# A post-norm decoder of two layers on one core: values, expert steps and the start of the self-attention in another order

## The chip, the core and the metric

The kernel runs on one core of one Trainium2 chip. The metric is the device time of one launch in microseconds; for this kernel it is the median of three runs. The core's engines run beside each other and meet at semaphores: TensorE (matmuls, results into eight PSUM banks of 2 KB per partition), VectorE, ScalarE, POOL (GpSimd) and SP (SyncE), which here only issues DMAs. DMAs are issued from SP's, ScalarE's and POOL's queues, each in the order of the program.

## What is computed

Four sequences of 512 tokens, width 256, pass through two layers; each sublayer is added to its input and normalized. All arithmetic is in 32-bit floats. Cut to what matters here:

```
x = LN(x + ttt(x))                       # layer 0: one inner SGD step per token
x = LN(x + attention(x, ctx, ctx, mask)) # one head, 1601 context rows per batch
p = softmax(x @ Wr + br); top 2 of 8 experts, weights w normalized to 1
x = LN(x + sum_k w_k * expert_k(x))      # expert: gelu(x Wi + bi) * sigmoid(x Wg + bg), Wo, LN
x = LN(x + causal_attention(x))          # layer 1: 16 heads of 16
Q, K = rope(x Wq + bq), rope(ctx Wk + bk); V = ctx Wv + bv
x = LN(x + softmax(Q K^T / 4) V Wo + bo) # 16 heads against 1601 context rows
x = LN(x + 0.5 * mlp(LN(x)))             # weights dequantized from integers
```

## The kernel before

The stages follow one another: layer 0's recurrence (to about 230 us of the span), its cross-attention (to about 530), the experts (to about 1001), layer 1's self-attention (to about 1440), its cross-attention (to about 2275) and the last block. Within a stage the program is a list of small Python closures called in an order written out by hand (`manual_schedule`), so each engine's instructions stand in that order, and a tile's reuse becomes a wait.

**The end of the first cross-attention.** While it ends, `value(b, k)` (L782) makes the value rows of layer 1's cross-attention for batches 2 and 3: 26 groups of 128 context rows, each of four TensorE instructions and a copy by ScalarE (L791). Two values share one two-bank tile of `wide()`; three such tiles and two one-bank tiles of `bank()` exist. When a batch's values are done, SP writes them to DRAM (`vd`, L793 to L797). Behind these on SP stand the loads of twelve weights and rows of layer 1 (L79, L92, L85), which go where the values lay, and then the experts' first rows `xb` (L922). Batch 3's routing and its scatter of rows run meanwhile.

**The experts.** `run` (L1110) goes through 19 blocks: eight "first" blocks, 256 rows of one expert each (weights loaded by SP), and eleven "more" blocks of two halves of 128 rows, each half of an expert found at run time (weights gathered by POOL). After `first_half` of a block, the second half of the block before follows, and then one step of the generator `attention_first` (L1019), which prepares layer 1: constants, tables, context columns of batch 0, masks. Attention needs, per batch, DRAM buffers `qd`, `ksd`, `kcd` of 32 rows per head, of which 16 come from projections and 16 are constants (`behind`, L877); these are copied from DRAM to DRAM on ScalarE's queue for all four batches, and then the mask rows (L1077). What is left of the generator runs behind the last block; then all engines meet at a branch (L1160).

**Behind the experts.** Eight PSUM banks are split into three of `spare()`, four of `one()` and one for the sums of weighted values. In this order come: gathers of batch 0's expert rows by POOL (L1223); values of batch 0 from context columns that lie in the tiles of queries and keys (`here=qt + kself`); two keys; values of batch 1 with the sums and the normalization of batch 0 (`add`) between the eighth and the ninth; transposes; keys; projection of first queries and keys (`self_rows`), which go through DRAM (L1202, L1205), since a row per head is to lie on other partitions; the rest of the keys. A key is copied by ScalarE (L1330) into one of four `raw` tiles and rotated by `rotated` (a shuffle and three products or sums). Rotated keys wait in the list `going` until `flush` issues their write.

Then come 16 self-attention units (batch, group of four heads) and 16 of cross-attention. A unit first runs its row maxima (`slot1`, TensorE and VectorE; 12 slots before the first unit), then scores, exponents and weighted sums. `extras[i]`, `quiet[i]` and `starts[i]` are lists of other closures that unit i runs between its own. The order before the first unit is:

```
for f in keys0[0:2] + values1[:8] + add + values1[8:] + turn + keys0[4:6]:
    f()
for f in (k0_, q0_, rows0, *keys0[2:4], *keys0[6:8], *self_values(0)):
    f()
cosT = const(p4c, "c_cos", [P, S2], nc.sync)
sinT = const(p4c, "c_sin", [P, S2], nc.sync)
flush(0)
```

`k0_`, `q0_`, `rows0` are the first half of batch 0's keys and queries and the loads of their rows; `k1_`, `q1_`, `rows1` the second half, which runs in unit 0.

Of the kernel before, what the change touches and what calls it, by code (L numbers as in the profile page):

```python
# [9 lines left out]
F32 = mybir.dt.float32  # L10
# [7 lines left out]
P = 128  # L18
# [7 lines left out]
NH, HD = 16, 16  # L26
# [13 lines left out]
def decoder(ctx: ExitStack, tc: tile.TileContext, a: dict, out: bass.AP):  # L40
# [14 lines left out]
    def wide():  # L55
        return psum["A"].tile([P, 2, 512], F32, tag="wide", name="wide")
# [571 lines left out]
    with tc.tile_pool(name="p2", bufs=2) as p2, ExitStack() as ordered:  # L628
# [135 lines left out]


        xaV = weight(p2, "xaV")
        values, places, halves = [], {}, []

        def rows_of_values(first):

# [10 lines left out]

        def value(b, k):  # L782
            kn = kn_of(k)
            if not halves or len(halves) == 2:
                halves[:] = [wide()]
            else:
                halves.append(halves[0])
            ps = halves[0][:, len(halves) - 1, :D]
            mm(ps[:kn], [(ctxTs[b][:, c, k * P : k * P + kn], xaV[:, c, :]) for c in range(2)])
            dst = places[b, k][:kn, : NH * VW].rearrange("p (h r) -> p h r", r=VW)  # L790
            nc.scalar.copy(dst[:, :, :HD], ps[:kn].rearrange("p (h r) -> p h r", r=HD))  # L791
            if (b, k) == (2, 8):
                nc.sync.dma_start(vd[2][:, : 9 * VROW], big_of(2, 0, 9))  # L793
            if (b, k) == (3, NKT - 1):
                nc.sync.dma_start(vd[3], big_of(3, 0, NKT))
            if (b, k) == (2, NKT - 1):
                nc.sync.dma_start(vd[2][:, 9 * VROW :], big_of(2, 9, NKT))  # L797

        def big_of(b, k0, k1):
            first = places[b, k0]  # L800
            return bass.AP(first.tensor, first.offset, [first.ap[0], [1, (k1 - k0) * VROW]])
# [72 lines left out]
    def by_head(t):  # L874
        return t.rearrange("(h r) n -> h r n", r=32)

    def behind(t, rows):  # L877

        nc.scalar.dma_start(by_head(t)[:, HD:, :], a[rows].rearrange("(h r) n -> h r n", r=HD))

    def group_tiles(pool, name, n):
        return [
# [11 lines left out]
    with tc.tile_pool(name="p3", bufs=2) as p3, ExitStack() as ordered:  # L894
# [124 lines left out]
        def attention_first():  # L1019
# [24 lines left out]
                    nc.scalar.dma_start(t, a[name][:, k0 : k0 + kw])  # L1044
                ready["turn", i] = pair
            yield
            for b in range(B):
                behind(qd[b], "c_rowq")
                behind(ksd[b], "c_rowks")
                yield  # L1050
            for b in range(B):
                behind(kcd[b], "c_rowkc")
                yield
            ngs = ready["ngs"] = []
            for i in range(2 * NT):
                t = p4a.tile([P, 4, 32], F32, tag=f"ng{i}", name=f"ng{i}")
# [7 lines left out]
            for c, k0 in enumerate(range(0, S2, 401)):  # L1064
# [8 lines left out]
                nc.sync.dma_start(mrow[:, k0 : k0 + kw], mf)  # L1073
                nc.vector.tensor_reduce(any_[:, c : c + 1], mf, AX.X, ALU.max)
                yield
            for b in range(B):
                nc.scalar.dma_start(  # L1077
                    by_head(kcd[b])[:, HD + 4, :], mrow[4 * b].partition_broadcast(NH)
                )
            yield  # L1080
            left = p3.tile([4 * B, 1], F32, tag="left", name="left", bufs=1)
            nc.vector.tensor_reduce(left, any_, AX.X, ALU.max)
# [57 lines left out]
                next(work, None)  # L1140
            second_half(blocks[-1], None, outs)

        order = "ffmfmfmmfmfmmfmfmm" + "m" * 1
        counts = {"f": iter(range(E)), "m": iter(range(NDYN // 2))}
        blocks = [({"f": "first", "m": "more"}[k], next(counts[k])) for k in order]
        def beside():
# [25 lines left out]
    with ExitStack() as s4:  # L1172
# [14 lines left out]
        def spare():  # L1187
            return ps2.tile([P, 512], F32, tag="s2", name="s2")

        def one():  # L1190
            return spare() if alone else ps1.tile([P, 512], F32, tag="one", name="one")

        diagq, later_, qt, kself, ngs, vself = (
            ready[k] for k in ("diagq", "later", "qt", "ks", "ngs", "vself")
# [67 lines left out]
            fetch = [lambda h=h: fetched(h) for h in range(2)]  # L1262
            return fetch, [lambda t=t: (added(t), stats(t)) for t in range(NT)] + ends, turns

        def self_rows(b, c):


            def item(name, dram, scale):
                ps = one()
                mm(ps, [(W[name][:, i, c * P : (c + 1) * P], xT[b][:, i, :]) for i in range(2)])  # L1270
                t = raw_tile()
                nc.scalar.activation(t, ps, AF.Identity, scale=scale)
                to_rows(dram, c, 0, S, t)

            def rows():
                for g in (2 * c, 2 * c + 1):
                    from_rows(kself, ksd[b], g)
                    from_rows(qt, qd[b], g)

            return [lambda: item("qkvK", ksd[b], 1.0), lambda: item("qkvQ", qd[b], QS)], rows  # L1280
# [40 lines left out]
        def context(b, keys, values, here=None):  # L1321


            def key(src, i, c, eng):
                flush(1)
                k0, kw = chunks[i]
                ps = one()
                mm(ps[:, :kw], [(W["xaK"][:, h, c * P : (c + 1) * P], src()[h][:, :kw]) for h in range(2)])
                raw = raw_tile()
                nc.scalar.activation(raw[:, :kw], ps[:, :kw], AF.Identity, bias=bkc[:, c : c + 1])  # L1330
                rotated(raw, kw, slice(k0, k0 + kw), eng, ready["turn", i] if here else None)
                going.append(lambda: to_rows(kcd[b], c, k0, kw, raw[:, :kw]))

            def value(src, k):
                kn, c0 = kn_of(k), (k % 4) * P
                ps = one()[:, :D]
                mm(ps[:kn], [(src()[c][:, c0 : c0 + kn], W["xaV"][:, c, :]) for c in range(2)])
                dst = vals[b % 2][:kn, k, : NH * VW].rearrange("p (h r) -> p h r", r=VW)
                nc.scalar.copy(dst[:, :, :HD], ps[:kn].rearrange("p (h r) -> p h r", r=HD))

            items = []
            for i in sorted({*keys, *values}):
                if here is None:
                    src = lambda n=len(stream): chunk(n)
                    stream.append((b, i))
                else:
                    src = lambda i=i: here[2 * i : 2 * i + 2]
                eng = nc.gpsimd if here is None else nc.vector
                if i in keys:
                    items += [lambda s=src, i=i, c=c: key(s, i, c, eng) for c in range(2)]  # L1350
                if i in values:
                    items += [lambda s=src, k=k: value(s, k) for k in range(4 * i, min(4 * i + 4, NKT))]
            return items
# [379 lines left out]
                starts[i + 1 + g].append(lambda b=b, g=g: from_rows(kcross, kcd[b], g))  # L1733


        fetch, add, turn = combined(0)
        values1 = context(1, (), range(4))
        keys1 = context(1, range(4), ())
        chunk(0)
        vals.append(values_tile(p4c, "v1", NKT))  # L1740
        for f in fetch:
            f()
        for f in first_sums:
# [2 lines left out]
            f()  # L1746
        nc.scalar.preload_act_table_set(EXP_AND_LN)

        keys0 = context(0, range(4), (), here=qt + kself)
        (k0_, q0_), rows0 = self_rows(0, 0)  # L1750
        (k1_, q1_), rows1 = self_rows(0, 1)

        for f in keys0[0:2] + values1[:8] + add + values1[8:] + turn + keys0[4:6]:
            f()
        for f in (k0_, q0_, rows0, *keys0[2:4], *keys0[6:8], *self_values(0)):
            f()
        cosT = const(p4c, "c_cos", [P, S2], nc.sync)
        sinT = const(p4c, "c_sin", [P, S2], nc.sync)
        flush(0)
        for i, (n0, n1) in enumerate(((0, 4), (4, 6), (6, 7), (7, 8))):  # L1760
            extras[i] = ([k1_, q1_, rows1] if i == 0 else []) + keys1[n0:n1] + extras[i]
        later = [context(2, range(4), ()), context(3, range(4), ())]
        for b in (2, 3):
            starts[index[b - 1, 1, True]].append(
# [2 lines left out]
        for b, work in enumerate(later):  # L1767
            for g in range(NG):
                n = -(-len(work) // (NG - g))
                extras[index[b, g, True]] += work[:n]  # L1770
                work = work[n:]

        nothing = lambda: None
        quiet[index[1, 0, True]].append(bias_out)
# [228 lines left out]
```

## Time and profile before

| | us |
|---|---|
| median of three runs (2403.08 to 2413.41) | 2409.47 |
| profiled execution | 2402.61 |
| its span, first to last instruction | 2400.8 |
| TensorE busy | 2275.6 |
| TensorE busy of the 420 us from 590 to 1010 (experts) | 394.1 |
| TensorE busy of the 50 us from 1010 to 1060 | 38.6 |
| TensorE busy of the 60 us from 1060 to 1120 | 59.0 |
| TensorE busy of the 1060 us from 1240 to 2300 | 1053.4 |

The span is that of one execution taken by the hardware profiler. An entry of a timeline gives start and length in us, the engine, the line of the kernel, the operation with its output and inputs, how many instructions are merged in it, and in brackets how long the engine was idle before it and what ended that. A row of stretches gives, for each engine, its busy time and the number of instructions. The granted clock is the share of full speed at which TensorE was allowed to run; over the whole span it was 0.97.

### The profile page before, as it was taken

The page shows a single profiled execution, that of the slowest core. Times are in us where ns is not written, and L with a number is a line of the kernel's source. Part 1 is how long each engine was busy: PE and PEld are TensorE (multiplying, and loading weights), DVE is VectorE, ACT ScalarE, POOL GpSimd, SP SyncE. Part 2 cuts the span into 40 slices and gives each one's busy share as a digit, 9 for nine tenths or more (in the row PEclk, how much of TensorE's full clock was granted, in tenths as well). Part 3 has the DMA queues.
Part 4 walks back from the last instruction along what each step waited for, and adds up shares of the span by engine and source line. Part 5 has one row for each costly group of instructions (what it writes and reads, how often), then busy time and mean ns, then how long its engine had stood idle before and what let it go on. Part 6 is the DMA issues. An engine that isn't in the chain of part 4 may idle for free.

```text
span 2400.8 us, 36163 instructions
## 1 busy us (share of the span) xinstructions
PE 2275.6 (95%) x14448; PEld 1289.9 (54%) x14448; DVE 1239.0 (52%) x2928; ACT 1064.2 (44%) x2103; POOL 360.0 (15%) x373
## 2 busy tenths in 40 slices
PE   7899999968999999889999999999999999999998
PEld 4767577757898988643333334333333333333266
DVE  1433234431333334356666667666766776677234
ACT  1111122213554545324555553655656566566730
POOL 1010001130122223225230010120122010000000
PEclk9999999988999999989999998999999999999999
DMA  8400311135887867341210210111110010100000
GB/s 304 173 0 1 132 55 46 45 137 178 321 333 308 338 258 300 132 147 50 67 49 27 77 64 1 37 33 59 56 58 28 25 60 15 54 11 20 30 10 27
DMA packets 77100, 244.14 MB, mean 102 GB/s; under 512 B 11640, under 2 KB 34686, under 8 KB 64638
## 3 DMA queue, kind: packets, MB, share of 16 engines
q1 hardware_dynamic: 60126, 137.41, 16.7%
q0 software_dynamic: 13632, 89.32, 9.7%
q10 hardware_dynamic: 3168, 15.03, 1.8%
q8 instruction: 116, 1.90, 0.3%
q14 instruction: 58, 0.48, 0.1%
HBM read 196.12 MB, written 56.77 MB: 105 GB/s over the span
## 4 chain that ended last, share of the span: by engine, by line
PE 50%; DVE 1%; ACT 1%; issue 0%; DVEq 0%; ACTq 0%
PE s L1458 23%; PE po L1485 12%; PE one L202 11%; PE s L202 2%; PE s L1468 1%; PE one L1443 1%; PE one L1506 1%; ACT x L171 0%; ACT ex L1472 0%; DVE pm L1415 0%; DVE one L1417 0%; PE one L1527 0%; PE one L1625 0%; PE one L1548 0%; DVE nb L166 0%
## 5 line engine op out<-in xcount | busy, mean ns | idle before, releaser
L1472 ACT ACTIVATE ex<-s 128x512 f32<-128x512 f32 (+1 forms) x1062 | 578.2, 594 | 458.2 <-PE s L1458 222.8
L1415 DVE TENSOR_REDUCE pm<-one 128x1 f32<-128x512 f32 x768 | 492.8, 685 | 159.5 <-PE s L1458 104.0
L1458 PE MATMUL s<-q,kc 32*128 32x512 f32 x1612 | 527.6, 638 | 0.8 <-ACT ex L1472 0.8
L202 PE MATMUL one<-kc,qt 32*128 32x512 f32 (+1 forms) x2048 | 482.5, 562 | 0.3 <-DVE pm L1415 0.3
L1458 PEld LDWEIGHTS s<-q,kc 32*128 32x128 f32 x1612 | 165.9, 179 | 202.5 <-issue 170.0
L1485 PE MATMUL po<-ex,v 128*32 128x256 f32 (+3 forms) x2688 | 250.9, 442 | 0.3 <-ACT ot L1498 0.3
L1417 DVE CUSTOM_DVE_ANT_0 one<-one,c_diagq 128x512 f32<-128x512 f32 x256 | 171.8, 716 | 76.0 <-PE one L202 65.1
L1485 PEld LDWEIGHTS po<-ex,v 128*32 128x32 f32 (+1 forms) x2688 | 54.1, 108 | 252.4 <-issue 244.9
L1458 PE MATMUL s<-q,ks 32*128 32x512 f32 x512 | 180.0, 650 | 5.3 <-ACT ex L1472 4.9
L202 PEld LDWEIGHTS one<-kc,qt 32*128 32x128 f32 x2048 | 164.2, 188 | 11.8 <-DVE pm L1415 7.8
L202 PE MATMUL bank<-eWo,g 128*128 128x256 f32 x608 | 141.9, 390 | 13.6 <-DVE rb L997 10.7
L202 PE MATMUL one<-ks,qt 32*128 32x512 f32 x512 | 149.7, 662 | 0.6 <-DVE pm L1417 0.6
L202 PE MATMUL wide<-xbT,eWi 128*128 128x128 f32 (+1 forms) x960 | 142.9, 310 | 4.0 <-DVE xbT L943 4.0
L202 PEld LDWEIGHTS wide<-xbT,eWi 128*128 128x128 f32 x960 | 132.9, 196 | 13.4 <-issue 3.4
L977 DVE TENSOR_TENSOR g<-g,sg 128x1024 f32<-128x1024 f32 x38 | 46.3, 1223 | 178.5 <-ACT sg L975 178.5
L202 PE MATMUL wide<-xbT,eWg 128*128 128x128 f32 (+1 forms) x960 | 137.0, 303 | 0.0
L202 PEld LDWEIGHTS bank<-eWo,g 128*128 128x128 f32 x608 | 116.4, 196 | 33.5 <-DVE rb L997 14.8
L1298 POOL TENSOR_TENSOR raw<-raw,c_cos 128x512 f32<-128x512 f32 (+1 forms) x32 | 35.0, 1094 | 654.8 <-DVE swp L1297 554.8
L202 PEld LDWEIGHTS wide<-xbT,eWg 128*128 128x128 f32 x960 | 128.1, 191 | 6.6
L1458 PEld LDWEIGHTS s<-q,ks 32*128 32x128 f32 x512 | 53.9, 185 | 83.3 <-issue 61.7
L202 PE MATMUL wide<-ctxT,q 128*128 128x512 f32 (+1 forms) x256 | 91.3, 510 | 0.8 <-DVE q L669 0.8
L975 ACT ACTIVATE g<-wide,eWi 128x128 f32<-128x128 f32 (+1 forms) x240 | 72.6, 415 | 27.0 <-PE wide L202 26.8
(326 smaller groups left out, 2943.0 us busy)
## 6 DMA issues: line engine op xcount, KB each, us to landing
xs<-zero SPq DMA_DIRECT2D x32, 512.0 KB
kc<-kcd SPq DMA_DIRECT2D x16, 800.5 KB
eWo<-in_eWo SPq DMA_DIRECT2D x8, 1408.0 KB
eWi<-in_eWi SPq DMA_DIRECT2D x8, 1028.0 KB
eWg<-in_eWg SPq DMA_DIRECT2D x8, 1028.0 KB
qt<-qd SPq DMA_DIRECT2D x32, 256.0 KB
ctxT<-in_ctxT SPq DMA_DIRECT2D x4, 1601.0 KB
kcd<-in_c_rowkc ACTq DMA_DIRECT2D x4, 1601.0 KB
```

The costliest lines, as they stand in the source:

```text
L202: nc.tensor.matmul(ps, l, r, start=(i == 0), stop=(i == n - 1))
L975: nc.scalar.activation(dst[:, k, :], pv[:, k, :], func, bias=bias)
L977: nc.vector.tensor_tensor(part, part, dst, ALU.mult)
L1298: eng.tensor_tensor(raw[:, :n], raw[:, :n], cos[:, :n], ALU.mult)
L1415: nc.vector.tensor_reduce(pm[:, t, j, c : c + 1], ps, AX.X, ALU.max)
L1417: nc.vector.tensor_tensor_reduce(out=ps, in0=ps, in1=diagq[:, 384 - t * P : 896 - t * P], scale=1.0, scalar=LOWEST, op0=ALU.add, op1=ALU.m ...
L1443: nc.tensor.transpose(pt[:, t * P : (t + 1) * P], ng.rearrange("p j r -> p (j r)"), ident)
L1458: nc.tensor.matmul(ps[:kn], kt[rows, k * P : k * P + kn], q2[rows, :], start=True, stop=cross)
L1468: nc.tensor.matmul(ps[:, k * P : (k + 1) * P], later_[:, :P], later_[:, P:], start=False, stop=True)
L1472: nc.scalar.activation(ex[:kn, h, :], ps[:kn], AF.Exp)
L1485: nc.tensor.matmul(state["po"][j * 32 : j * 32 + 32, q0:q1], (vals if cross else vself)[b % 2][:kn, k, c0 : c0 + 32], ex[:kn, j % 2, q0:q1 ...
L1506: nc.tensor.transpose(pt[:, t * P : (t + 1) * P], ot[:, t * P : (t + 1) * P], ident)
```

## The change

Five things are done.

1. A value of batches 2 and 3 takes two tiles of `bank()` and one of `wide()` by turns, one value each, and the writes to `vd` are issued by ScalarE.
2. In `attention_first` the constant rows of `qd`, `ksd`, `kcd` and the mask rows are written for batch 0 alone; those of the other batches are written from SP's queue (`rows_behind`), batch 1's before the first unit, batch 2's and 3's at the start of units 4, 6, 8 and 10.
3. The order of the expert blocks has the first blocks a little later.
4. Until the first unit starts, `one()` takes three of every seven tiles from `spare()`.
5. Behind the experts the four keys of two chunks are multiplied and copied first, then come the sums of batch 0 and its normalization, and only then the rotations of these keys. The first keys and queries go into tiles of tag `q2` and not into `raw`; of batch 1's values three stand before the transposes, six behind, and four go into units 0 and 1; the other four keys of batch 0 go into unit 0, those of the odd chunks rotated on POOL; batch 1's keys move from units 0 to 3 to units 1 to 3. The constant part of batch 1's value tile is set by VectorE and not by POOL.

```diff
         def value(b, k):
             kn = kn_of(k)
-            if not halves or len(halves) == 2:
-                halves[:] = [wide()]
-            else:
-                halves.append(halves[0])
-            ps = halves[0][:, len(halves) - 1, :D]
+            turns[0] += 1
+            ps = wide()[:, 0, :D] if turns[0] % 3 == 0 else bank()[:, :D]
...
             if (b, k) == (2, 8):
-                nc.sync.dma_start(vd[2][:, : 9 * VROW], big_of(2, 0, 9))
+                nc.scalar.dma_start(vd[2][:, : 9 * VROW], big_of(2, 0, 9))
...
-    def behind(t, rows):
-
-        nc.scalar.dma_start(by_head(t)[:, HD:, :], a[rows].rearrange("(h r) n -> h r n", r=HD))
+    def behind(t, rows, queue=nc.scalar):
+
+        queue.dma_start(by_head(t)[:, HD:, :], a[rows].rearrange("(h r) n -> h r n", r=HD))
+
+    def masked(b, queue=nc.scalar):
+        queue.dma_start(by_head(kcd[b])[:, HD + 4, :], mrow[4 * b].partition_broadcast(NH))
...
-            for b in range(B):
-                behind(qd[b], "c_rowq")
-                behind(ksd[b], "c_rowks")
-                yield
-            for b in range(B):
-                behind(kcd[b], "c_rowkc")
-                yield
+            behind(qd[0], "c_rowq")
+            behind(ksd[0], "c_rowks")
+            yield
+            behind(kcd[0], "c_rowkc")
+            yield
...
-            for b in range(B):
-                nc.scalar.dma_start(
-                    by_head(kcd[b])[:, HD + 4, :], mrow[4 * b].partition_broadcast(NH)
-                )
+            masked(0)
...
-        order = "ffmfmfmmfmfmmfmfmm" + "m" * 1
+        order = "ffmfmmfmfmmfmfmmf" + "m" * 2
...
+        all_banks = [True]
+
         def one():
-            return spare() if alone else ps1.tile([P, 512], F32, tag="one", name="one")
+            if all_banks:
+                all_banks.append(True)
+            if alone or len(all_banks) % 7 in (2, 4, 6):
+                return spare()
+            return ps1.tile([P, 512], F32, tag="one", name="one")
...
-                rotated(raw, kw, slice(k0, k0 + kw), eng, ready["turn", i] if here else None)
-                going.append(lambda: to_rows(kcd[b], c, k0, kw, raw[:, :kw]))
+                turn = lambda: rotated(raw, kw, slice(k0, k0 + kw), eng, ready["turn", i] if here else None)
+                write = lambda: to_rows(kcd[b], c, k0, kw, raw[:, :kw])
+                if apart is None:
+                    turn()
+                    going.append(write)
+                else:
+                    apart.append(lambda: (turn(), write()))
...
-                eng = nc.gpsimd if here is None else nc.vector
+                eng = nc.gpsimd if here is None or i % 2 else nc.vector
...
+        def rows_behind(b, queries, keys, behind=behind):
+            if queries:
+                behind(qd[b], "c_rowq", nc.sync)
+                behind(ksd[b], "c_rowks", nc.sync)
+            if keys:
+                behind(kcd[b], "c_rowkc", nc.sync)
+                masked(b, nc.sync)
+
...
-        vals.append(values_tile(p4c, "v1", NKT))
+        vals.append(values_tile(p4c, "v1", NKT, nc.vector))
...
-        (k0_, q0_), rows0 = self_rows(0, 0)
+        (k0_, q0_), rows0 = self_rows(
+            0, 0, lambda: p4.tile([P, S], F32, tag="q2", name="q2")
+        )
         (k1_, q1_), rows1 = self_rows(0, 1)
-
-        for f in keys0[0:2] + values1[:8] + add + values1[8:] + turn + keys0[4:6]:
-            f()
-        for f in (k0_, q0_, rows0, *keys0[2:4], *keys0[6:8], *self_values(0)):
-            f()
+        turns0 = []
+        for f in keys0[0:2] + keys0[4:6]:
+            f(turns0)
+        for f in add + turns0 + values1[:3] + turn + [k0_, q0_, rows0] + self_values(0) + values1[3:9]:
+            f()
+        all_banks.clear()
         cosT = const(p4c, "c_cos", [P, S2], nc.sync)
         sinT = const(p4c, "c_sin", [P, S2], nc.sync)
-        flush(0)
-        for i, (n0, n1) in enumerate(((0, 4), (4, 6), (6, 7), (7, 8))):
-            extras[i] = ([k1_, q1_, rows1] if i == 0 else []) + keys1[n0:n1] + extras[i]
+        rows_behind(1, True, True)
+
+        extras[0] = [
+            k1_, q1_, *keys0[2:4], lambda: (keys0[6](), keys0[7]()), lambda: (flush(0), rows1()),
+            *values1[9:11],
+        ] + extras[0]
+        extras[1] = values1[11:] + keys1[:2] + extras[1]
+        for i, n in enumerate((2, 5)):
+            extras[i + 2] = keys1[n : n + 3] + extras[i + 2]
...
+        for i, what in ((4, (2, True, False)), (6, (2, False, True)), (8, (3, True, False)), (10, (3, False, True))):
+            starts[i].append(lambda what=what: rows_behind(*what))
```

## The prediction

> **What bounds the kernel now.** I read the page first, then the stretches of the span, then TensorE's own timeline with the idle time before each entry.
>
> ```profile
> span 2400.8 us, 36163 instructions
> PE 2275.6 (95%) x14448; PEld 1289.9 (54%) x14448; DVE 1239.0 (52%) x2928; ACT 1064.2 (44%) x2103; POOL 360.0 (15%) x373
> PE 50%; DVE 1%; ACT 1%; issue 0%; DVEq 0%; ACTq 0%
> ```
>
> TensorE is busy 95% of the span and the chain of waits is nearly all matmuls. The change removes no matmul, so it can only win idle TensorE time (125 us in all) or time at the half clock. It touches three places, and there the timeline of TensorE reads:
>
> ```profile
> 510.37 1.99 PE L202 MATMUL wide<-xaV,ctxT 128*128 128x256 f32 x8 [0.46 <-ACT v L791]
> 512.83 1.99 PE L202 MATMUL wide<-xaV,ctxT 128*128 128x256 f32 x8 [0.46 <-ACT v L791]
> ...
> 546.81 1.08 PE L939 MATMUL bank<-ident,xb 128*128 128x128 f32 x4 [18.22 <-DMA xb<-xs]
> ...
> 768.01 0.63 PE L939 MATMUL bank<-ident,xb 128*128 128x128 f32 x4 [3.46 <-DMA xb<-xs]
> ...
> 1001.38 9.07 PE L202 MATMUL one<-xaV,qt 128*128 128x256 f32 x32 [3.00 <-PEq L1160]
> ...
> 1033.56 1.97 PE L202 MATMUL one<-xaV,cx 128*65 128x256 f32 x4 [4.24 <-ACT v L1339]
> ...
> 1058.20 3.78 PE L202 MATMUL one<-qkvV,xT 128*128 128x256 f32 x8 [5.10 <-ACT raw L1330]
> 1061.91 2.06 PE L202 MATMUL one<-ks,qt 32*128 32x512 f32 x8
> ```
>
> The bracket is the wait and its releaser. In the stretches behind the experts the last three columns are granted clock, DMA share and GB/s:
>
> ```profile
> 1030.00:1040.00 10.00, 6.44 (x17) 3.96 (x18) 0.56 (x1) 5.18 (x13) 7.82 (x10) 0.66 0.44 132
> 1050.00:1060.00 10.00, 3.37 (x11) 2.13 (x10) 5.58 (x15) 1.62 (x5) 0.00 (x0) 0.82 0.61 195
> 1070.00:1080.00 10.00, 9.42 (x28) 2.96 (x21) 5.84 (x20) 0.85 (x2) 0.00 (x0) 0.68 0.61 174
> ```
>
> TensorE idles 3.6 and 6.6 us in the first two, and the clock is low in each.
>
> **A. The values at the end of the first cross-attention.** Two values (2 x 4 matmuls) share one wide tile and wait 0.46 us for the copy of the pair before: 2.46 us a pair by the starts above. Without the wait 32 such matmuls take 7.07 us (the values of batch 1 at 1018.04), so 0.88 us a value. With bank, bank, wide by turns a value waits for the copy (0.37 us) of the third before it: covered. From 507.92 the last 17 values take 20.7 us; after, 17 x 0.88 = 15.0, plus 1.3 for two banks which the routing sums hold until VectorE has read them (last at 509.3). That is 4.4 won, and about 1.2 in the six values ahead of it: 5.6 us. Does it reach the end? After the last copy (529.0) SP issues the last vd write at 529.03, then waits for it until 531.87, issues twelve weight loads and only then xb at 543.54, which ends the 18.22 us. All of this hangs on the last copy and keeps its length, so the whole block moves. The vd writes change from SP to ScalarE's queue behind the same copies: two issues of 0.34 us between copies, hidden by the bank slack. The next to be late would be the scatter of batch 3 (last issue 518.3 on POOL), 20 us ahead of xb: not reached. **-5.6** (ends 0 and -8).
>
> **B. The experts.** (1) Nine of twelve constant copies from DRAM to DRAM (each batch: 0.5 MB c_rowq, 0.5 MB c_rowks, 1.6 MB c_rowkc) and three mask rows leave ScalarE's queue: 8.4 MB less beside 117 MB. TensorE waited for xb four times (0.85, 0.74, 1.29, 3.46 us: 6.3). The longest was issued at 754.26, 2.4 us behind a c_rowkc copy, and took 13.7 us; two others also follow constants. I take 4.5 of the 6.3; ends 0 and 6.3. (2) The steps beside the experts shrink from 21 to 15, so none is left behind the last of 19 blocks. Now the tail runs xaO,bv (993.69), VectorE, a one-row matmul (997.69) and bob until 998.84, and all engines start 2.5 us later. After, the last VectorE work is the experts' own, until 997.31: -1.5. (3) The order of blocks keeps 8 first and 11 pair blocks and their matmuls. The mask steps come six blocks earlier; their stalls (3.02 us before 862.37, 3.15 before 910.03, VectorE waiting for the mask's DMA while the second half of a pair block waits for VectorE) have the same form at their new places: 0, ends +4 and -4. **-6.0**.
>
> **C. Behind the experts.** Now 60.5 us pass from 1001.38 to the first scores at 1061.91. After, in today's clock times:
> - POOL loses a memset (0.7 us) ahead of its gathers, VectorE gains it. The sums follow the gathers and are done by about 1016, long before they were (1029.6).
> - The square root stands on ScalarE behind four key copies. TensorE ends the 13 values at 1014.7, as now; seven banks keep them from waiting. Four keys at 1.8 (3.60 for two) end at 1021.9, the fourth copy (0.69) at 1022.6. Root and apply take 0.3 + 0.2 + 0.56 + 2.07 with hops: x is ready at 1026.1 (now 1033.3). TensorE has three values to do meanwhile and idles about 1.9, then 0.9 behind its transposes.
> - First key and query: 1.88 each, copied into own tiles by 1033.3. But SP has four kcd writes ahead of them, and these wait for four rotations on VectorE, 2.71 each (1040.86 to 1043.57), from 1023.9 to 1034.8, the sums now standing first. So ksd goes at 1035.2 and qd at 1035.8 (now 1044.19 and 1045.91).
> - qd's write to the issue of qt's read took 5.2 us (1045.91 to 1051.14): 1041.0, and about 3 more to land, estimated from ksd's 3.5.
> - TensorE's values run out: value 8 reads a chunk whose load stands on SP behind the four row loads, so 1045; the scores start near **1046**, after a wait of some 4.5 us.
>
> That is 16 us earlier. Put off into the first units are four values (3.5), two keys (3.6) and two short ones (1.0): 8.1, which TensorE pays later, since there it goes from item to item. (The odd chunks' keys rotate on POOL, 3 x 1.28 us each, instead of 3 x 0.69 on VectorE; POOL stood idle from 1040 to 1080.) Net -7.8.
>
> What this adds: c_cos, c_sin and batch 1's constants (4.4 MB) go on SP ahead of ksd and qd of the second half. c_cos with c_sin took 9 us from the issue at 1056.65, by the high GB/s until 1066; the other 2.8 MB are estimated at 7 to 9 from the 336 to 441 GB/s between 639 and 651, when two such copies ran among weights. The mask row goes into the tile that c_rowkc fills, so SP waits there until about 1060 (1044 + 9 + 7). Behind it: ksd, qd; for their tiles (four raw buffers) wait the short keys' copies on ScalarE, for these a shuffle on VectorE, for it the maxima, and for those TensorE. Needed near 1061.5, free near 1064.5: **+3** (ends 0 and +12). Batches 2 and 3 come a unit (23 us) before use: 0.
>
> Here a rule speaks against the change: by the Trainium skill (DMA: Bandwidth & Descriptors, Queues, rings and completion order) an engine takes turns between queue rows but keeps order within one. On ScalarE's row the constants would cost ksd little, on SP's ksd stands behind all: 0 against my +3. The trace shows only their own row, where xb still took 13.7 us.
>
> Clock: the skill (TensorE: Matmul & The Clock Gate, HAM oscillation) says a gap above about 3.4 us throttles, and a cold stretch loses half its time. The waits of 4.24 and 5.10 agree (8 matmuls of the second took 3.78, not 1.8). But 3.02 at 862.37 was also followed by slow matmuls (5.17 for 3.72) and 3.46 at 768.01 was not; by the rule B's saved wait would bring 1.7 more, by the row nothing, and I take the row. Of four low stretches behind the experts I let one go, and keep one for the wait of 4.5: **-2.5** (ends +3 and -9).
>
> C: -7.8 + 3 - 2.5 = **-7.3**. Sum: -5.6 - 6.0 - 7.3 = **-18.9 us**. From the profiled execution (2402.61) 2383.7; that one lies 6.9 under the median of the three runs (2409.47), from which it is 2390.6. The reported time being a median, I say **2390**.
>
> **Rivals.**
> 1. *Everything lands* (0.2): all xb waits, both mask stalls and three cold stretches go: -5.6 in A, -6.3 - 1.5 - 4 in B, -7.8 - 7.5 in C, together -33, so 2376. For it: each cold stretch follows a gap. Against: the wait for rows through DRAM stays.
> 2. *Hidden anyway* (0.22): A holds, but xb is late for the experts' own weights, and the earlier start is paid back in the first units, where keys now rotate on POOL beside its sums: about -7, so 2402. For it: POOL stands behind gathers, the raw tiles are four.
> 3. *Slower* (0.12): SP's wait at the mask row. If 4.4 MB land not near 1060 but by T, all engines stand T - 1060 longer. From T = 1079 (130 GB/s) the 19 us are gone, and from 1092 (some 93 GB/s) the kernel takes 2422, 0.5% more. For it: four engines in a row hang on one write, and xb's 0.26 MB took 13.7 us beside such copies. Against: the 336 to 441 GB/s.
>
> That the change does less than it says is no rival: issue orders move as described.
>
> **Numbers.** Forecast 0.46, rivals 0.2, 0.22, 0.12. 0.5%, about what a measurement of this kernel tells from no change, is 12 us: under 2397 is faster, over 2421 slower. Faster: 0.44 + 0.2 + 0.02 = 0.66; same 0.22; slower 0.12. The forecast's ends and rival 1 give 2373, rival 2 with its spread 2406.
>
> **What would show it.** A: no 0.46 waits at the values, xb's transpose near 541. B: no xb wait above 1.5 us and the stage's start some 12 us earlier in all. C: scores 45 us, not 60, behind the first values; one stretch under 0.85. The forecast is wrong if the span to the first values shrinks by under 6, or if a copy waits on ksd's write for over 10 us.

## The result, and the profile after

The changed kernel takes **2394.45 us** (median of 20 runs, 2386.76 to 2402.17), the kernel before 2404.26 (median of 20 runs, its first three among them). The ratio is **0.9952, 95% interval 0.9942 to 0.9963**: 0.5% faster. The profiled execution took 2391.23 us, its span is 11.7 us shorter than before. From the page:

```profile
span 2389.1 us, 36156 instructions
PE 2270.9 (95%) x14448; PEld 1287.5 (54%) x14448; DVE 1231.9 (52%) x2918; ACT 1063.0 (44%) x2103; POOL 369.3 (15%) x383
PE 53%; ACT 1%; DVE 1%; DMA 1%; POOL 1%; issue 0%; SPq 0%; DVEq 0%; ACTq 0%; POOLq 0%
```

TensorE does the same 14448 matmuls, and what the chain accounts for is still nearly all TensorE (53 of some 58%). TensorE's timeline at the three places:

```profile
517.47 1.13 PE L202 MATMUL bank<-xaV,ctxT 128*128 128x256 f32 x4 [0.40 <-ACT v L788]
518.44 1.03 PE L202 MATMUL wide<-xaV,ctxT 128*128 128x256 f32 x4
522.49 1.94 PE L202 MATMUL bank<-xaV,ctxT 128*65 128x256 f32 x8 [3.02 <-ACT v L788]
...
546.00 1.09 PE L939 MATMUL bank<-ident,xb 128*128 128x128 f32 x4 [18.98 <-DMA xb<-xs]
...
607.02 0.63 PE L939 MATMUL bank<-ident,xb 128*128 128x128 f32 x4 [2.15 <-DMA xb<-xs]
673.70 0.63 PE L939 MATMUL bank<-ident,xb 128*128 128x128 f32 x4 [1.27 <-DMA xb<-xs]
746.61 5.25 PE L202 MATMUL bank<-eWo,g 128*128 128x256 f32 x16 [3.31 <-DVE rb L997]
980.51 5.38 PE L202 MATMUL bank<-eWo,g 128*128 128x256 f32 x16 [3.31 <-DMA eWo<-in_eWo,wrow]
988.15 1.59 PE L202 MATMUL s<-xaV,qt 128*128 128x256 f32 x4 [2.26 <-ACTq L1155]
...
1036.51 2.05 PE L202 MATMUL one<-xaV,cx 128*128 128x256 f32 x4 [11.30 <-DMA cx<-in_ctxT]
1038.49 2.06 PE L202 MATMUL one<-ks,qt 32*128 32x512 f32 x8
...
1122.40 3.35 PE L202 MATMUL one<-cx,xaK 128*128 128x512 f32 x4 [3.37 <-DMA cx<-in_ctxT]
```

At the values (first three lines) the regular 0.46 us waits are gone, but two irregular ones came, of 0.40 and 3.02; xb's transposes stand 0.8 us earlier. In the experts two long waits for xb are left of four, one stall at the mask of two, and the next stage starts 2.3 us behind the last matmuls (985.89), not 7.6. Behind the experts one wait of 11.30 us for a context chunk stands ahead of the first scores, and a new one at 1122. The span therefore divides so:

| from, to | before | after | |
|---|---|---|---|
| start, xb's transposes | 546.8 | 546.0 | -0.8 |
| to the next stage's start | 454.6 | 442.2 | -12.4 |
| to the first scores | 60.5 | 50.3 | -10.2 |
| to the end | 1338.9 | 1350.6 | +11.7 |

SP's timeline shows why the chunk is late (issue, length):

```profile
1022.55 0.58 SPq L1203 DMA_DIRECT2D ksd<-q  x1
1023.22 0.58 SPq L1203 DMA_DIRECT2D qd<-q  x1
1027.39 0.34 SPq L1206 DMA_DIRECT2D ks<-ksd  x1
1028.95 0.34 SPq L1206 DMA_DIRECT2D qt<-qd  x1
...
1030.34 0.93 SPq L1316 DMA_DIRECT2D cx<-in_ctxT  x2
1031.32 0.66 SPq L861 DMA_DIRECT2D c_cos<-in_c_cos  x1
...
1034.47 0.59 SPq L876 DMA_DIRECT2D kcd<-in_c_rowkc  x1
1048.38 0.50 SPq L879 DMA_DIRECT2D kcd<-mrow  x1
```

The chunk's load goes only when the row reads, which wait for ksd's and qd's writes, are issued; 1 MB of rows is ahead of it and 4.4 MB of constants behind it, and it lands 6.2 us later. The row of stretches from 1030 on (busy PE, PEld, DVE, ACT, POOL, then granted clock, DMA share, GB/s) has TensorE at 3.49 of 10 us and the clock at half:

```profile
1030.00:1040.00 10.00, 3.49 (x12) 2.19 (x12) 0.00 (x0) 0.37 (x1) 3.27 (x4) 0.51 0.98 352
```

### The profile page after: what moved, and what is told of

The parts are those of the page before. It is cut to its first block, busy times and chain, and to the rows that moved or that the text cites. A ratio compares the mean times of both kernels' runs of the same rounds, so it can differ in the third digit from the quotient of the medians.

```text
span 2389.1 us, 36156 instructions
## 1 busy us (share of the span) xinstructions
PE 2270.9 (95%) x14448; PEld 1287.5 (54%) x14448; DVE 1231.9 (52%) x2918; ACT 1063.0 (44%) x2103; POOL 369.3 (15%) x383
## 4 chain that ended last, share of the span: by engine, by line
PE 53%; ACT 1%; DVE 1%; DMA 1%; POOL 1%; issue 0%; SPq 0%; DVEq 0%; ACTq 0%; POOLq 0%
PE s L1467 23%; PE one L202 12%; PE po L1494 12%; PE s L202 3%; PE s L1477 1%; PE one L1452 1%; PE one L1515 1%; DMA cx<-in_ctxT 1%; ACT x L171 1%; DVE one L1426 0%; ACT ex L1481 0%; DMA y<-ys,yrows 0%; DVE pm L1424 0%; PE one L1536 0%; DMA qd<-q 0%
```

## The experiments

Twelve kernels ran, in three groups of four on one chip each; each is the changed kernel with the edit shown, and its ratio is against the kernel before on the same chip. The changed kernel itself was not run again on these chips, so a difference of some us between it and a run (a1 and b1 stand 6 and 7 us under it) need not be all due to the edit; runs of one group can be compared directly. The lengths are from one profile each: from the issue of batch 2's first vd write to batch 3's, the experts (xb's transposes to the next stage's start), from there to the first scores, and from these to the end.

| kernel | ratio (95%) | vd writes | experts | to scores | to end |
|---|---|---|---|---|---|
| before | 1 | 16.28 | 454.6 | 60.5 | 1338.9 |
| changed | 0.9952 (0.9942-0.9963) | 16.40 | 442.2 | 50.3 | 1350.6 |
| c1_chunk_first | 0.9918 (0.9891-0.9945) | 15.29 | 442.4 | 47.4 | 1349.8 |
| c3_writes_behind | 0.9938 (0.9919-0.9957) | 15.66 | 442.6 | 53.7 | 1350.2 |
| c4_both | 0.9915 (0.9893-0.9936) | 15.59 | 439.7 | 39.0 | 1359.3 |
| c2_burst_later | 0.9929 (0.9906-0.9952) | 15.74 | 439.2 | 52.7 | 1351.6 |
| d1_both_burst_later | 0.9871 (0.9842-0.9899) | 12.50 | 442.2 | 38.3 | 1348.9 |
| d2_chunks_on_scalar | 0.9855 (0.9826-0.9883) | 12.51 | 441.5 | 39.1 | 1344.3 |
| a1_vd_on_sp | 0.9928 (0.9902-0.9954) | 12.50 | 439.8 | 49.9 | 1353.2 |
| a2_values_as_before | 0.9947 (0.9928-0.9966) | 16.27 | 442.2 | 50.3 | 1355.3 |
| b1_order_as_before | 0.9923 (0.9900-0.9945) | 12.49 | 442.4 | 49.1 | 1349.4 |
| b2_constants_back | 0.9958 (0.9944-0.9972) | 12.50 | 452.4 | 49.9 | 1351.6 |
| b3_constants_same_steps | 0.9997 (0.9984-1.0011) | 12.50 | 462.1 | 49.5 | 1351.2 |
| e_all | 0.9832 (0.9809-0.9855) | 12.50 | 441.6 | 39.1 | 1340.3 |

### What holds the first scores

c1_chunk_first:

```
-for f in add + turns0 + values1[:3] + turn + [k0_, q0_, rows0] + self_values(0) + values1[3:9]:
+for f in add + turns0 + values1[:5] + turn + [k0_, q0_, rows0] + self_values(0) + values1[5:9]:
```

> Five values of batch 1 instead of three stand ahead of the transposes of x, so that the load of the third context chunk is issued on SP behind the four kcd writes but ahead of ksd, qd and the row reads. Everything else as in the changed kernel (2394.5 us, stage start to first scores 50.3 us, of which 11.3 us are a wait for that chunk). Theory 1 (the chunk's place on SP holds the first scores): the wait for cx goes, TensorE then waits only for the first rows of qt, whose read is issued 40.8 us behind the stage's start and lands about 3 us later: scores at +44 to +46, 4 to 6 us earlier, total 2388.5 to 2390.5. Theory 2 (the rows through DRAM would be as late anyway): the scores move by under 1.5 us, total 2393 to 2396. Theory 3 (the two values put ahead delay the transposes and so the first key and query): scores later by 1 to 2 us, total 2395 to 2397.

The scores came at +47.4 (a plus sign: us behind the stage's start). The wait for the chunk fell from 11.30 to 2.97 us, and 3.58 us of it returned as a wait for qt:

```profile
1027.31 2.04 PE L202 MATMUL one<-xaV,cx 128*128 128x256 f32 x4 [2.97 <-DMA cx<-in_ctxT]
1032.92 2.09 PE L202 MATMUL one<-ks,qt 32*128 32x512 f32 x8 [3.58 <-DMA qt<-qd]
```

From qd's write to the issue of qt's read it took 7.6 us here, not 5.7. The chunk's 0.5 MB stands ahead of them here, but c2, where it doesn't, took 6.9, so that cause isn't shown. A part of theory 1: the place on SP matters, but the rows bind next.

c3_writes_behind (a turn and its write are kept apart, and the four writes follow the rows):

```
-apart.append(lambda: (turn(), write()))
+apart.append((turn, write))
...
-for f in add + turns0 + values1[:3] + turn + [k0_, q0_, rows0] + self_values(0) + values1[3:9]:
+writes0 = [w for _, w in turns0]
+turns0 = [t for t, _ in turns0]
+for f in add + turns0 + values1[:3] + turn + [k0_, q0_, rows0] + writes0 + self_values(0) + values1[3:9]:
```

> The four kcd writes of the first keys of batch 0, on which SP stands until 34 us behind the stage's start, are issued behind the rows of the first key and query instead of ahead of them; the rotations keep their place on VectorE. Theory 1 (SP's order holds the rows and the chunk): ksd goes as soon as its copy is there, about +29, qt's reads at about +35 and the chunk's load behind them at about +37, landing at +40 to +42; the first scores come at +41 to +44, 6 to 9 us earlier, total 2385.5 to 2388.5. Theory 2 (what is won at the start is paid back in the first units, where rotations and writes stand late): scores earlier by as much, the time from the first scores to the end longer by 5 us or more, total 2392 to 2395. Theory 3 (the chunk is held by the burst of the constants and not by SP's order): scores earlier by under 3 us, total 2392 to 2394.

The rows went early (qt's read at +37.4, from 40.8), yet the scores came at +53.7. The chunk, now behind the kcd writes too, was issued at +42.7 and landed 9.0 us later, beside them and the constants. A miss for theory 1: half of the cure only moved the wait.

c4_both has the two edits together.

> Both edits: chunk load and first rows ahead of the four kcd writes. Theory 1: no wait for the chunk at all, the values fill TensorE until about +37, then it waits for the first rows of qt, read at about +35: first scores at +38 to +40, 10 to 12 us earlier than in the changed kernel, total 2382.5 to 2385. Theory 2 (paid back in the first units): 2390 to 2394. Theory 3 (burst): as the writes alone, within 1.5 us of that run.

The scores came at +39.0, as theory 1 has it; but 8.7 us were given back behind them. TensorE, SP, then ScalarE and VectorE of this run, in that order:

```profile
1023.98 1.14 PE L202 MATMUL one<-ks,qt 32*128 32x512 f32 x8 [2.73 <-DMA qt<-qd]
...
1052.18 1.19 PE L1467 MATMUL s<-q,ks 32*128 32x512 f32 x1 [7.92 <-DVE q L1456]
```

```profile
1044.17 0.50 SPq L879 DMA_DIRECT2D kcd<-mrow  x1
1044.77 0.65 SPq L1203 DMA_DIRECT2D ksd<-raw  x1
1045.56 0.62 SPq L1203 DMA_DIRECT2D qd<-raw  x1
```

```profile
1049.15 0.32 ACT L1332 ACTIVATE raw<-s,bk 128x65 f32<-128x65 f32 x1 [9.86 <-DMA ksd<-raw]
1049.58 0.01 DVE L1298 LOAD_MASK_SELECT swp<-raw  x1 [6.29 <-ACT raw L1332]
```

This is the chain that the prediction feared in its third rival: SP stands at the mask row until c_rowkc has landed, ksd and qd stand behind it, the short keys' copy on ScalarE waits 9.86 us for their raw tiles, VectorE waits for the copy and TensorE 7.92 us for VectorE. In the changed kernel SP stands 13.2 us at the mask row, and TensorE waits 1.30 us at that place (1059.55); c2, which issues the 4.4 MB of constants later, waits 1.51. So nothing of the 13.2 us is seen there: the late scores were their cover.

c2_burst_later:

```
-cosT = const(p4c, "c_cos", [P, S2], nc.sync)
-sinT = const(p4c, "c_sin", [P, S2], nc.sync)
-rows_behind(1, True, True)
+def late():
+    trig["cos"] = const(p4c, "c_cos", [P, S2], nc.sync)
+    trig["sin"] = const(p4c, "c_sin", [P, S2], nc.sync)
+    rows_behind(1, True, True)
+starts[1].append(late)
```

> The 4.4 MB of constants (c_cos, c_sin, batch 1's rows and mask row) are issued on SP at the start of the second unit instead of ahead of the first. Theory 1 (the chunk's place on SP holds the scores): the chunk still goes at +42 and lands 3 to 4 us later, not 6, scores at +47 to +48; SP's wait of 13.2 us at the mask row moves to the second unit; total 2390 to 2393. Theory 2 (the burst is what made the chunk late and TensorE's clock low): scores at +45 or before and the stretch behind them at full clock, total 2386 to 2389. Theory 3 (the constants are then late for batch 1's keys and rows): new waits in the second and third units, total 2396 or more.

The scores came at +52.7, later than any theory had them, and TensorE waited 12.33 us for the chunk (SP's issue, then TensorE):

```profile
1029.84 0.90 SPq L1316 DMA_DIRECT2D cx<-in_ctxT  x2
1034.65 2.04 PE L202 MATMUL one<-xaV,cx 128*128 128x256 f32 x4 [12.33 <-DMA cx<-in_ctxT]
```

The load landed in 4.8 us instead of 6.2, but SP issued it at +46.0 instead of +42.2. Up to there the program is the changed kernel's, yet ksd went at +37.0, not +34.4; why is open. So the burst is worth some 1.4 us of the landing and is not what makes the chunk late; theory 2 falls. (b2 and b3, below, have only c_cos and c_sin there, and their scores come at +49.9 and +49.5.) Nor was anything late in the next units (theory 3).

d1_both_burst_later joins these three edits.

> Chunk load and first rows ahead of the four kcd writes, and the 4.4 MB of constants behind the first unit. In the run with the first two edits alone the scores began 39.0 us behind the stage's start, not 50.3, but TensorE then stood 7.9 us at 1052: SP waited 13 us for c_rowkc at the mask row, ksd and qd of the second key and query stood behind it, and ScalarE waited 9.9 us for their tiles. Theory 1 (that wait is the constants' burst on SP): without the burst ahead of them ksd and qd go when copied, no wait above 2 us in the first unit, scores at +38 to +39, total 7 to 8 us under the run with the two edits: 2377 to 2380 where the kernel before takes 2408. Theory 2 (the rows of the second half are late anyway, for TensorE runs ahead of VectorE): a wait of 4 us or more stays near there, total 2382 to 2386. Theory 3 (the burst, moved, collides with the first unit's keys): new waits in the second unit, total 2384 or more.

Scores at +38.3 and no wait above 1.2 us in the first unit; 2372.28 us where the kernel before takes 2403.48 on this chip, a ratio of 0.9871, which is 2377 of the 2408 in the expectation. Theory 1 holds: the stall of c4_both was the burst on SP (10.4 us less behind the scores by the profiles). Of the time between the two runs some 3 us are the values' copies, below.

d2_chunks_on_scalar is d1 with one word more:

```
-nc.sync.dma_start(
+nc.scalar.dma_start(
     t[:, :, :kw], a["ctxT"][b].rearrange("(c p) k -> p c k", p=P)[:, :, k0 : k0 + kw]
```

> As the run beside it, and the loads of the context chunks are issued on ScalarE's queue instead of SP's. In every run with the change's key distribution TensorE waits 3.3 to 4.4 us in the third unit for a chunk whose load stands on SP behind kcd writes that wait for POOL's rotations, and the eight matmuls behind it take twice their time (3.35 us for 1.72). Theory 1 (SP's order makes that wait): both go, 4 to 6 us less than the run beside it. Theory 2 (POOL's rotations are late, and the next wait is for the raw tiles): the wait changes its name and keeps 2 us or more; less than 2 us gained. Theory 3 (loads on ScalarE hold up its exponentials): slower by 2 us or more.

The wait in the third unit and the slow matmuls behind it (4.24 us and 3.55 for 1.94 in d1) are gone, and the time behind the first scores is 4.6 us shorter: theory 1 by the profile, though the medians differ by only 3.4 us and the intervals overlap. The premise needs mending: in the changed kernel the chunk awaited at 1122.40 was issued at 1115.70, behind one kcd write but above all behind the second rows' writes and reads (1106.90 to 1114.59), and it took 6.7 us to land.

### What the values brought

a1_vd_on_sp has `nc.sync` for `nc.scalar` at the three vd writes.

> The changed kernel with the three vd writes back on SP's queue; banks by turns stay. In all five profiles with the change ScalarE's copies of the values stall 7 to 8 us behind the first vd write (four idle spells of 1.0 to 2.5 us while their banks are ready), so that the vd write of batch 3 goes 15.3 to 16.4 us behind that of batch 2, as before the change (16.28). Theory 1 (issuing the writes on ScalarE's queue stalls its copies): with SP issuing them the stalls go, batch 3's write comes 12.0 to 13.0 us behind batch 2's, xb 3 to 4 us earlier, total about 2391 by the former comparison (2394.5 for the changed kernel). Theory 2 (the stalls belong to the scatter's indirect DMAs of POOL that run beside them, or to the banks by turns): the same stalls stay, time within 1 us of the changed kernel.

a2_values_as_before has that and the pairs in one wide tile again.

> The changed kernel with the values of the first cross-attention as before: pairs in one wide tile, vd writes on SP. Theory 1 (the values' new banks brought next to nothing, since the copies stall on ScalarE): the 0.46 us waits come back, xb's transposes 38.9 us behind batch 2's vd write instead of 37.9 to 38.4, total 0 to 1.5 us above the changed kernel. Theory 2 (the forecast's 5.6 us are there, hidden by a spread between executions): 4 to 6 us above it.

In a1 the stalls are gone and the two writes 12.50 us apart, as theory 1 expected. But it can't be theory 1: d1, d2, b1, b2 and b3 issue the writes on ScalarE and have the same 12.5 us without a stall. ScalarE in b1:

```profile
502.09 0.37 ACTq L790 DMA_DIRECT2D vd<-v  x1
503.49 0.37 ACT L788 COPY v<-bank 128x256 f32<-128x256 f32 x1 [1.43 <-PE bank L202]
504.69 0.38 ACT L788 COPY v<-bank 128x256 f32<-128x256 f32 x1 [0.82 <-PE bank L202]
505.55 0.38 ACT L788 COPY v<-wide 128x256 f32<-128x256 f32 x1 [0.49 <-PE wide L202]
...
514.58 0.33 ACTq L792 DMA_DIRECT2D vd<-v  x1
```

And in the changed kernel's own profile, where the copies idle for 2.15, 2.51 and 1.76 us with their banks full (by the order of the matmuls these tiles were full at 515.3, 516.2 and 517.1):

```profile
514.52 0.37 ACT L788 COPY v<-bank 128x256 f32<-128x256 f32 x1 [0.49 <-issue]
517.04 0.37 ACT L788 COPY v<-bank 128x256 f32<-128x256 f32 x1 [2.15 <-PE wide L202]
519.92 0.37 ACT L788 COPY v<-wide 128x256 f32<-128x256 f32 x1 [2.51 <-PE wide L202]
522.06 0.65 ACT L788 COPY v<-bank 128x256 f32<-128x256 f32 x2 [1.76 <-remote]
```

The stall is in the profiles of the changed kernel and of c1 to c4 (the first group, one chip), and in none of the other seven with banks by turns. The scatter's DMAs run beside all of them, so theory 2's causes don't tell them apart either. What makes it is open. Where it is absent the values bring 3.2 to 3.9 us up to xb (35.0 to 35.7 us from batch 2's write, where before has 38.9 and a2 39.0), where it is present 0.4 to 1.0. By time, a2's ratio is that of the changed kernel, 0.9947 beside 0.9952. Against a1 on the same chip a2 takes 4.2 us more (medians 2390.93 and 2386.68, ranges overlapping), which agrees with the 3.9 us of their profiles.

### What the experts gained from

b1_order_as_before:

```
-order = "ffmfmmfmfmmfmfmmf" + "m" * 2
+order = "ffmfmfmmfmfmmfmfmm" + "m" * 1
```

> The changed kernel with the former order of the expert blocks; the 15 steps beside them and everything else stay. In nine profiles with the new order the experts take 439.2 to 442.6 us from the first transposes of xb to the next stage's start (454.6 before the change), with one stall at the mask's DMA of 3.2 to 3.6 us where there were two. Theory 1 (the order is worth nothing, as forecast): 439 to 443 us, total within 1.5 us of the changed kernel. Theory 2 (the order spared one mask stall with the slow matmuls behind it, 3.15 + 1.5 us): two stalls again, 443.5 to 447 us, total 3 to 5 us above it.

442.4 us: the order is worth nothing by the stage's length, though two mask stalls returned (3.11 and 2.55 us); b1 has less waiting for xb beside them (1.43 us, 3.42 in the changed kernel), and these waits differ from run to run (1.2 to 3.7 us in sum with the new order). The total lies some 7 us under the changed kernel's by the ratios, more than theory 1 allows; about 3 of them are the values, whose copies do not stall in this group, and the intervals overlap.

b2_constants_back and b3_constants_same_steps both drop `rows_behind` behind the experts and put all batches' copies beside them; b3 issues them in the first batch's two steps:

```
 for b in range(B):
     behind(qd[b], "c_rowq")
     behind(ksd[b], "c_rowks")
-    yield
+yield
 for b in range(B):
     behind(kcd[b], "c_rowkc")
-    yield
+yield
```

> The changed kernel with all twelve constant copies and the four mask rows back on ScalarE's queue beside the experts, in 21 steps as before the change; nothing of them comes on SP behind the experts except c_cos and c_sin. Theory 1 (the step count made the tail, the copies the waits for xb): 5 to 6 us from the end of the last block's matmuls to the next stage return, xb waits sum to 5 to 6.5 us instead of 2 to 3.4, so the experts take 449 to 453 us; the first scores come as early behind the stage's start as in the run with the burst moved (52 to 53 us) and SP's wait at the mask row is gone; total 2398 to 2403 by the former comparison, where the changed kernel takes 2394.5. Theory 2 (the copies cost nothing there): experts 439 to 446 us, total 2390 to 2395.

452.4 us: theory 1. The xb waits sum to 6.6 us (3.4 in the changed kernel), and the tail is back, in TensorE's timeline:

```profile
985.52 1.02 PE L202 MATMUL bank<-xaO,bv 128*1 128x256 f32 x4
989.51 0.69 PE L202 MATMUL bank<-xa_bo,ones 1*128 1x256 f32 x2 [2.97 <-DVE xa_bo L1096]
993.21 2.05 PE L202 MATMUL s<-xaV,qt 128*128 128x256 f32 x4 [3.00 <-PEq L1158]
```

Two waits of 3 us with two small matmuls: 7.6 us from the end of the last block to the next stage, where the changed kernel has 2.3. The stage is 10.0 us longer than b1's. Against b1 on the same chip the kernel takes 10.8 us more (2393.53 and 2382.76).

> As the run beside it, but all four batches' copies in the steps of the first batch's, so 15 steps in all, as in the changed kernel. Theory 1 (the number of steps, not the bytes, makes the tail): tail of 2.3 us as in the changed kernel, xb waits of 4 us or more in the blocks beside the copies, experts 443 to 447 us, total within 2.5 us of the changed kernel. Theory 2 (the bytes make it: the copies pile up and xb or the weights come late block after block): experts 449 us or more, total 4 us or more above it.

The tail is 2.3 us, so the number of steps makes it. But theory 2 holds for the bytes, by more than it said:

```profile
659.50 9.58 PE L202 MATMUL wide<-xbT,eWi 128*128 128x128 f32 x64 [4.63 <-DMA eWi<-in_eWi,wrow]
679.80 9.66 PE L202 MATMUL wide<-xbT,eWg 128*128 128x128 f32 x64 [10.72 <-DMA eWg<-in_eWg,wrow]
```

Twelve copies at once hold the experts' own weights by 15 us, and the kernel is no faster than before (0.9997). Spreading the copies over more steps, as before the change, costs the tail of 5.4 us and saves 15; moving nine of them out of the stage, as the change does, saves both.

### All that helped

e_all is d2 with the vd writes on SP and three more values ahead of the first scores (empty steps keep the units' other items in their places):

```
-... writes0 + self_values(0) + values1[5:9]:
+... writes0 + self_values(0) + values1[5:12]:
```

> The best of the runs so far (chunk loads on ScalarE, first rows ahead of the kcd writes, constants behind the first unit: 0.9855 of the kernel before) with two more edits: the vd writes on SP, and three more values of batch 1, whose chunk is there, ahead of the first scores, where TensorE waited 2.9 us for qt. Theory 1 (that wait is idle time which the values fill): the wait for qt falls under 0.5 us, the scores stand as early as before (39 us behind the stage's start) and the units behind are 2.6 us shorter: 2 to 3 us under that run, about 0.984 to 0.985. Theory 2 (the first units are bound by VectorE's maxima and not by TensorE): no gain from the values, within 1 us of that run.

The wait for qt fell from 2.88 to 0.28 us with the scores at +39.1, and the rest is 4.0 us shorter:

```profile
1022.80 1.30 PE L202 MATMUL one<-ks,qt 32*128 32x512 f32 x8 [0.28 <-DMA qt<-qd]
```

**2364.3 us, 0.9832 of the kernel before (0.9809 to 0.9855)**: it beats both, and its interval lies below the changed kernel's by more than either is wide.

## Why the prediction was right, and where it was not

The forecast of 2390 is 4.5 us under the measured median, and the range holds it. That closeness is in good part luck. The sum was -18.9 us, and -9.8 were measured between the medians (-11.7 between the profiles). 2390 was reckoned from 2409.47, the median of three runs; over twenty the kernel before takes 2404.26, from which the sum gives 2385.4. And the terms were off on both sides, so that their errors cancel in part.

- **A, -5.6: measured -0.8.** The size of the matmuls' share was nearly right: without stalls the 17 values save 3.8 us (16.28 to 12.50 between the writes), where 4.4 was said. Two things failed. "All of this hangs on the last copy and keeps its length" is wrong: SP's first weight load comes 7.70 us behind the *issue of batch 3's vd write* before (524.17 to 531.87), 7.37 after and 7.67 in b1. That 1.9 MB write binds, not the last copy (from the last write's issue to the load it is 2.84, 3.92 and 4.22 us), so the wait for xb grows from 18.22 to 19.5 to 20.2 us in the unstalled runs and 3.2 to 3.9 are left. And ScalarE's stalled copies, which nothing in the profile of before announced, took most of that in the changed kernel's profile. Moving the writes to ScalarE's queue brought nothing, as said. Batch 3's write and the first weight load behind it, in the kernel before and in the changed one:

```profile
524.17 0.34 SPq L795 DMA_DIRECT2D vd<-v  x1
531.87 0.38 SPq L79 DMA_DIRECT2D qkvQ<-in_qkvQ  x1
```

```profile
524.00 0.33 ACTq L792 DMA_DIRECT2D vd<-v  x1
531.37 0.37 SPq L79 DMA_DIRECT2D qkvQ<-in_qkvQ  x1
```

- **B, -6.0: measured -12.4.** The waits for xb gave 2.9 of the 4.5; b2 loses 3.2 in them. The tail was the mis-sized term: -1.5 said, -5.4 measured, and the same by b2. It was argued that the stage can't end before VectorE's last expert work at 997.31. The stage does not wait for that: VectorE is at work on the last sums until 989.4 while TensorE already runs the next stage's values from 988.15. The block order is 0, as said (b1). One mask stall less with the slow matmuls behind it makes up the rest, 4.3 by the lines; but b1 has two and the same total, so that share isn't settled. Constants and steps together are worth 10.0 (b2 beside b1).
- **C, -7.3: measured +1.5** (-10.2 and +11.7). SP's times were good: ksd's write +33.8 said and +34.4 found, qt's read +39.6 and +40.8. The term that failed is the chunk: value 8 was put at +44, it came at +48.4, and the scores at +50.3 instead of +45. The load was priced as if it landed in about 3 us; it took 6.2 behind 1 MB of rows and beside the constants (4.8 without these in c2, 9.0 behind four more writes in c3). The wait that was said to be 4.5 us is 11.3, and TensorE idled at half the clock. Behind the scores 8.1 us of put-off work were to be paid; 11.7 were, and 4.6 of them went when the chunk loads left SP's queue (d2). That is rival 2's "paid back in the first units", by SP's order more than by POOL.
- **The mask row, +3:** nothing seen. The mechanism is real and its price depends on cover: 7.9 us as soon as the scores come 11 us earlier (c4). Rival 3's end was not reached, since the 4.4 MB landed by 1048 at 352 GB/s.
- **Clock:** one stretch under 0.85 was said; of the first nine stretches of 10 us behind the experts two are (0.51 and 0.66), where before had six, which the prediction counted as four; a third of 0.83 comes at 1120, with the new wait.

The measured time lies between the forecast and rival 2. Neither case that was named as proof against the forecast came: the span to the first values shrank by 13.2 us, not by under 6, and no copy waited over 10 us on ksd's write. But a sign failed in each part: xb's transposes came at 546.0, not near 541, a wait for xb of 2.15 us is left where none above 1.5 was to be, the scores came 50 us behind the first values, not 45, and two stretches, not one, are at a low clock.

## What to carry to other kernels

A DMA queue is an order of work like an engine's: list what stands on it ahead of each load that someone will wait for, and give the load that ends the wait the first place or another queue; in this kernel three reorderings on SP and one change of queue brought 17.8 us (2368.87 in d2; 2386.68 in a1, which has none of them, ran on the same chip and has no stalled copies either), more than the change itself did. Size a load by what is on the engines when it is issued, not by its quietest landing. And when a stage is made to start earlier, look for the waits that its lateness covered: removing one wait alone often buys only the next (c1, c3, c4), and the gain came when all three went together.

## What the runs showed of the hardware

- **A gap of 3.3 us slows TensorE or not.** The 16 matmuls of the last expert block follow a wait for their weights or for VectorE. In the fourteen profiles they took 3.69 us after gaps of 2.75, 3.24, 3.34 and 3.38 us (b2, a1, c4, a2), and 5.20 to 6.68 us after the ten others, which run from 2.92 (before) to 3.73 (c3), with 3.27 (b3) and 3.31 (changed) among them. Even a stall of 2.57 us at the mask was followed by 5.24 us (b2), and one of 2.55 by 3.72 (b1). So between 2.6 and 3.4 us the length alone doesn't decide. The Trainium skill (TensorE: Matmul & The Clock Gate, What's actually happening) has the activity window free-running, which fits; the cost was 1.7 us in five profiles, half of the 3.4 us window given there, and 1.5 to 3.0 in the other five.
- **ScalarE can stall on copies whose banks are full**, which puts 2.8 to 3.9 us between the two writes, in every profile of one group and in the changed kernel's, and in none of the other two groups, for the same instructions; no row names a releaser that explains it (one says only "remote").
